# Layer 0's norm by DVE's statistics instructions, in a kernel of four graph attention layers

## The chip, the cores and the metric

The kernel runs on one core of a Trainium2 chip. The metric is the device time of that core in microseconds (us), as a median of several executions; lower is better. A core has five engines with a queue each, which they work off in order: TensorE (PE; its weight loads are listed apart as PEld), VectorE (DVE), ScalarE (ACT), GpSimd (POOL) and SyncE (SP, which issues DMAs). They wait for each other through semaphores.

## The reference

16 graphs of 1024 nodes with 256 features each go through four layers of graph attention. Each layer first normalizes the rows of x, cuts them at zero, projects them, forms attention weights over the edges, and adds the result to x. Cut to what matters here:

```python
def _layernorm(x, axis=-1, eps=1e-5):
    m = jnp.mean(x, axis=axis, keepdims=True)
    v = jnp.var(x, axis=axis, keepdims=True)
    return (x - m) / jnp.sqrt(v + eps)

# --- layer 0 (adj_preln) ---
h = jnp.maximum(_layernorm(x, axis=-1), 0.0)
x = x + _L0_gnn_ref(h, adj, L0_gnn_W, L0_gnn_a)
# layers 1, 2 and 3 have the same form, each with an attention of its own

# _L0_gnn_ref
Wh = jnp.einsum('bnf,fo->bno', h, W)
e = jax.nn.leaky_relu(f1[:, :, None] + f2[:, None, :], negative_slope=SLOPE)
e = jnp.where(adj == 0, NEG_INF, e)
attention = jax.nn.softmax(e, axis=-1)
h_prime = jnp.einsum('bij,bjo->bio', attention, Wh)
```

x is float32 of 16 x 1024 x 256, adj int32 of 16 x 1024 x 1024.

## The kernel before

A batch (one graph) is `xb`, 8 tiles of 128 nodes by 256 features, held in SBUF through all four layers. A layer has two parts. The projection (`project`, L267) works on a pair of tiles at a time: it finds the mean and the squares of each row, writes `centered` (row minus mean, cut at zero; the division by the deviation comes later), transposes it on TensorE (L290), copies it out of PSUM as `hT` on ACT (L292), multiplies it with W (L297), and hands each tile's product with `rstd`, the row's inverse deviation, to an eviction. The eviction of layers 0 and 1 takes an exponential on ACT (L361) and writes the values V on DVE (L365). The attention (`attend`, L393) transposes a column of V into a row (L314), makes eight tiles of weights of 128 x 1024 on DVE (L318), and multiplies them with V on TensorE (L409), two rows of results while the weights come and six afterwards. As results come (`finish0` L446, `add_elu` L336), x is updated on DVE with an instruction that also gives the row sums of the new x (`sums`), and every second tile starts the next layer's projection of that pair. So layers 1 to 3 get their sums along with the update. Layer 0 has no update ahead of it: `first` (L460) takes its sums from xb with a reduction of its own (L461), one over each pair.

From the sums, `project` makes `minus_mean` on DVE (L271), `centered` with it on DVE (L274), and the sum of squares on ACT (L281): a Square with the bias minus_mean, whose accumulator is read into `squared`. `inverse_root` (L257) adds the epsilon (L260) and raises to the power of -1/2 (L261), both on POOL. Layer 3 has four heads, whose sums are made with the weights as the moving operand (L517), copied (L579), turned back (L586, L594), and normalized again, head by head: L487 on POOL, L488 to L492 on DVE, the squares L494 on ACT, L496 on DVE, `inverse_root` on POOL, L500 on DVE, L501 and L502 on POOL; then the batch goes out (L611).

Two streams of batches run interleaved, the even ones and the odd ones. `stream` (L618) and the loop at L627 set the order of the text: each part yields a duration, and the stream with the least sum goes on; the second starts 111 units behind. So one stream's layer 3 and its next batch's layer 0 lie beside the other's layers 0 to 2. On each engine instructions keep the order that was fixed when the program was built; it need not be that of the text, save where `keep_in_program_order` says so.

Buffers are handed out by name: `minus_mean`, `squared`, `rstd2` and `sums_of_x` have six each, `centered` and `hT` three, `square` one, V four, x_b three. Except for the sums, all these names are shared by the layers and by both streams. The accumulators in PSUM (`acc0`, `acc1`) have two buffers for each stream. x_b is fetched by SP (L104), one megabyte a batch.

Of the kernel before, what the change touches and what calls it, by code (L numbers as in the profile page):

```python
# [32 lines left out]
F32 = mybir.dt.float32  # L33
BF = mybir.dt.bfloat16
# [3 lines left out]
AF = mybir.ActivationFunctionType  # L38
ALU = mybir.AluOpType
AX = mybir.AxisListType  # L40

P = 128
# [3 lines left out]
LN_EPS = 1e-5  # L46
# [13 lines left out]
def short_path(ctx: ExitStack, tc: tile.TileContext, ins: dict, out: bass.AP, bad: bass.AP):  # L60

    nc = tc.nc
    x, adj = ins["x"], ins["adj"]
    B, N, D = x.shape
    H, T, E = ins["L3_a_src"].shape
    NI = N // P
# [84 lines left out]
    work = ctx.enter_context(tc.tile_pool(name="work", bufs=3))  # L151
    small = ctx.enter_context(tc.tile_pool(name="small", bufs=6))
# [5 lines left out]
    bias = const.tile([P, D], F32, name="bias")  # L158
# [95 lines left out]

    def inverse_root(squared: bass.AP, n: int, elements: int, eps: float) -> bass.AP:  # L257

        r = small.tile([P, n], F32, name=f"rstd{n}")
        nc.gpsimd.tensor_scalar_add(r, squared, elements * eps)  # L260
        nc.gpsimd.tensor_tensor(r, r, minus_half.to_broadcast([P, n]), op=ALU.pow)  # L261
        return r

    def accumulator(b: int) -> bass.AP:
        return psum.tile([P, HALF], F32, name=f"acc{b % 2}")

    def project(b: int, l: int, xb: bass.AP, sums: bass.AP, pair: int, evict):  # L267


        minus_mean = small.tile([P, 2], F32, name="minus_mean")  # L270
        nc.vector.tensor_scalar_mul(minus_mean, sums[:, ts(pair, 2)], -1.0 / D)  # L271
        centered = work.tile([P, 2, D], F32, name="centered", bufs=3)
        for n in range(2):
            nc.vector.tensor_scalar(  # L274
                centered[:, n, :], xb[:, 2 * pair + n, :], minus_mean[:, n : n + 1], 0.0,
                op0=ALU.add, op1=ALU.max,
            )
        squared = small.tile([P, 2], F32, name="squared")
        for n in range(2):
            square = work.tile([P, D], BF, name="square", bufs=1)  # L280
            nc.scalar.activation(  # L281
                square, xb[:, 2 * pair + n, :], AF.Square, bias=minus_mean[:, n : n + 1],
                accum_out=squared[:, n : n + 1],
            )
        rstd = inverse_root(squared, 2, D, LN_EPS)
        yield 0.5
        turned = psum.tile([P, NK, 2 * P], F32, name="misc")
        for n in range(2):
            for k in range(NK):
                nc.tensor.transpose(turned[:, k, ts(n, P)], centered[:, n, ts(k, P)], ident)  # L290
        hT = wide.tile([P, NK, 2 * P], F32, name="hT", bufs=3)
        nc.scalar.mul(hT, turned, ROOT_D)  # L292
        yield 1.0
        for n in range(2):
            projected = accumulator(b)[:, : D + EXT[l]]
            for k in range(NK):
                nc.tensor.matmul(  # L297
                    projected, hT[:, k, ts(n, P)], W[l][:, k, :],
                    start=(k == 0), stop=(k == NK - 1),
                )  # L300
            evict(2 * pair + n, projected, rstd[:, n : n + 1])
        yield 2.5
# [46 lines left out]
    def batch(b: int):  # L349
        xb = xs.pop(b)  # L350
# [5 lines left out]
        def begin(l: int):  # L356

            V = nodes.tile([P, NI, H, E + 1], F32, name="V", bufs=4).rearrange("p i h e -> p i (h e)")

            def evict(i: int, projected: bass.AP, rstd: bass.AP):  # L360
                nc.scalar.activation(V[:, i, D : D + 3], projected[:, D:], AF.Exp, scale=rstd)  # L361
                if l == 2:
                    nc.scalar.mul(V[:, i, :D], projected[:, :D], rstd)
                else:
                    nc.vector.tensor_scalar(  # L365
                        V[:, i, :D], projected[:, :D], rstd, V[:, i, D : D + 1],
                        op0=ALU.mult, op1=ALU.mult,
                    )

            return V, evict  # L370
# [22 lines left out]
        def attend(l: int, V: bass.AP, finish, then: int):  # L393
# [35 lines left out]
            for i in range(NI):  # L429
                if i > 1:  # L430
                    for j in range(NI):
                        product(i, j)
                acc = accs.pop(i)
                finish(i, acc, sums[:, i : i + 1])
                if i != 0:
                    yield 3.6
                if i % 2 == 1:

                    yield from steps
                    steps = project(b, then, xb, sums, i // 2, following[1])  # L440
                yield from islice(steps, 1)
# [13 lines left out]
            add_elu(xb[:, i, :], acc, total)  # L455

        V, evict = begin(0)
        sums = small.tile([P, NI], F32, name="sums_of_x")

        def first(pair: int):  # L460
            nc.vector.tensor_reduce(sums[:, ts(pair, 2)], xb[:, ts(pair, 2), :], AX.X, ALU.add)  # L461
            yield from project(b, 0, xb, sums, pair, evict)

        pairs = [first(pair) for pair in range(NI // 2)]
        for n in range(NI // 2 + 2):
            for pair in range(max(n - 2, 0), min(n + 1, NI // 2)):
                yield from islice(pairs[pair], 1)
# [15 lines left out]
        def center(h: int):  # L483

            yh = y[:, :, h, :]
            head = ts(h, E)
            nc.gpsimd.tensor_add(yh, yh, bias[:, head].unsqueeze(1).to_broadcast(shape))  # L487
            nc.vector.scalar_tensor_tensor(yh, yh, 0.0, h3[:, :, head], op0=ALU.max, op1=ALU.add)  # L488
            mean = small.tile([P, NI], F32, name="mean")
            nc.vector.tensor_reduce(mean, yh, AX.X, ALU.add)  # L490
            nc.vector.tensor_scalar_mul(mean, mean, 1.0 / E)
            nc.vector.tensor_sub(yh, yh, mean.unsqueeze(2).to_broadcast(shape))  # L492
            square = wide.tile(shape, F32, name="wide", bufs=1)
            nc.scalar.activation(square, yh, AF.Square)  # L494
            var = small.tile([P, NI], F32, name="var")
            nc.vector.tensor_reduce(var, square, AX.X, ALU.add)  # L496
            return yh, head, inverse_root(var, NI, E, L3_EPS)
# [16 lines left out]
        def in_tiles(parts, accT: bass.AP, first: bool, last: bool):  # L514

            for n, (values, moving) in enumerate(parts):
                made = nc.tensor.matmul(  # L517
                    accT[ts(n, QUAD), :], values, moving, start=first, stop=last
                )

                if pinned:
                    tc.keep_in_program_order(made)
                pinned.append(made)
# [24 lines left out]
        for h in range(H):  # L548
# [16 lines left out]
            for first in range(0, NI, step):  # L565
                pinned = []
                for j in range(first, first + step, 2):
                    add_totals(h, j)
                    if h > 0:
                        add_values(h, j)  # L570
                for _ in range(step):
                    next(behind, None)
                yield 1.8 if h == 0 else 5.4
# [8 lines left out]
            sums, totals = copies if h == 0 else copies[::-1]  # L582
# [35 lines left out]
    def stream(first: int):  # L618
        for _ in loading[first]:
            yield 2.0  # L620
        for b in range(first, B, 2):
            yield from batch(b)
# [389 lines left out]
```

## Time and profile before

| What | Value |
|---|---|
| Median of three executions | 3025.95 us (3025.94 to 3026.56) |
| The profiled execution | 3025.06 us |
| Its span, first to last instruction | 3023.3 us |
| TensorE busy | 2905.2 us, 96% |
| DVE busy | 2112.7 us, 70% |
| ACT busy | 1092.1 us, 36% |
| POOL busy | 964.5 us, 32% |
| Mean granted TensorE clock | 0.993 |
| Layer 0's sums (L461) | 64 of 674 ns |
| minus_mean (L271), all layers | 256 of 189 ns |
| centered (L274), all layers | 512, median 347 ns |
| Squares (L281), all layers | 512 of 506 ns, and 512 accumulator reads of 191 ns |
| The two parts of inverse_root on POOL for 128x2 | 233 ns (L260) and 787 ns (L261) |

The profile is of one execution. Busy time is the time in which an engine works on an instruction; waits in its queue aren't counted. A group of instructions has its line, its engine, what it writes and reads, its count and mean duration; what stands in brackets behind an instruction in a timeline is the idle time of its engine ahead of it and what ended that. The chain that ended last is followed back from the last instruction, at each step to what released it. A quarter of each all-layer group belongs to layer 0.

### The profile page before, as it was taken

How to read it: one execution, taken by the hardware profiler on the slowest of the kernel's cores; microseconds unless marked ns; L12 is line 12 of the kernel's file. 1: busy time of each engine (PE TensorE's matmuls, PEld its weight loads, DVE VectorE, ACT ScalarE, POOL GpSimd, SP SyncE). 2: the span in 40 equal slices, each digit the busy share in tenths (PEclk: the TensorE clock that was granted, in tenths of full speed). 3: DMA queues.
4: the chain of work that ended last, by engine and by line, in shares of the span. 5: the costliest groups of instructions: out<-in, count | busy, mean ns of one | idle time of the engine just before them, and what ended most of it. 6: DMA issues, size and time to landing. Idle time of an engine off the chain costs nothing.

```text
span 3023.3 us, 44588 instructions
## 1 busy us (share of the span) xinstructions
PE 2905.2 (96%) x16774; PEld 1960.1 (65%) x16774; DVE 2112.7 (70%) x4467; ACT 1092.1 (36%) x3009; POOL 964.5 (32%) x1455
## 2 busy tenths in 40 slices
PE   7999999999999999999999999999999999999985
PEld 5775857658576675756758566585766857667551
DVE  5657687676866758677576875758667686675756
ACT  2333424243343433424334243433434334243331
POOL 2124324142232423324233242432324234242333
PEclk9999999999999999999999999999999999999997
DMA  7204023030321403122040220302204031110101
GB/s 122 37 8 63 29 29 56 8 49 29 36 49 14 71 2 49 36 28 57 5 50 31 29 56 8 50 29 32 53 11 56 19 50 36 15 29 5 19 21 30
DMA packets 120495, 106.11 MB, mean 35 GB/s; under 512 B 73680, under 2 KB 91216, under 8 KB 120272
## 3 DMA queue, kind: packets, MB, share of 16 engines
q0 software_dynamic: 40448, 67.12, 15.2%
q1 hardware_dynamic: 79824, 36.05, 5.9%
q8 instruction: 135, 2.21, 0.3%
q14 instruction: 88, 0.72, 0.1%
HBM read 153.49 MB, written 33.55 MB: 62 GB/s over the span
## 4 chain that ended last, share of the span: by engine, by line
PE 78%; DVE 12%; POOL 4%; ACT 4%; issue 2%; DMA 1%; SPq 0%; ACTq 0%; POOLq 0%; DVEq 0%
PE acc L409 39%; PE acc L517 21%; PE acc L297 11%; DVE weights L318 6%; PE misc L290 3%; PE row L314 2%; POOL rstd L261 2%; POOL y L487 1%; DVE y L500 1%; DVE V L365 1%; DVE var L496 1%; PE misc L594 1%; ACT adj_i L143 1%; ACT square L281 1%; PE misc L586 1%
## 5 line engine op out<-in xcount | busy, mean ns | idle before, releaser
L409 PE MATMUL acc<-V,weights 128*128 128x257 f32 x6144 | 1452.5, 386 | 24.6 <-ACT above L343 12.8
L409 PEld LDWEIGHTS acc<-V,weights 128*128 128x128 f32 x6144 | 1135.1, 190 | 338.3 <-DVE weights L318 92.7
L517 PE MATMUL acc<-weights,V 128*32 128x512 f32 x6144 | 756.4, 598 | 3.6 <-DVE weights L318 3.6
L318 DVE SCALAR_TENSOR_TENSOR weights<-row,ex,mask 128x1024 f32<-128x1024 f32 x512 | 631.2, 1276 | 91.0 <-PE acc L517 51.0
L297 PE MATMUL acc<-W,hT 128*128 128x259 f32 (+1 forms) x2048 | 522.1, 391 | 39.8 <-ACT hT L292 28.2
L297 PEld LDWEIGHTS acc<-W,hT 128*128 128x128 f32 x2048 | 376.5, 190 | 165.2 <-issue 49.5
L318 DVE SCALAR_TENSOR_TENSOR weights<-row,V,mask 128x1024 f32<-128x1024 f32 x384 | 475.4, 1276 | 7.7 <-PE row L314 7.7
L517 PEld LDWEIGHTS acc<-weights,V 128*32 128x32 f32 x6144 | 174.1, 109 | 379.6 <-issue 370.6
L341 ACT ACTIVATE below<-acc,inv 128x256 f32<-128x256 f32 x256 | 121.3, 474 | 681.0 <-DVE inv L334 404.1
L261 POOL TENSOR_TENSOR rstd<-rstd,minus_half 128x2 f32<-128x2 f32 (+1 forms) x320 | 307.7, 962 | 20.3
L281 ACT ACTIVATE square<-x_b,minus_mean 128x256 bf16<-128x256 f32 x512 | 259.2, 506 | 136.4 <-DVE minus_mean L271 131.7
L333 DVE TENSOR_SCALAR inv<-acc 128x1 f32<-128x1 f32 x256 | 39.7, 155 | 302.5 <-PE acc L409 299.0
L389 POOL TENSOR_TENSOR x_b<-x_b,beta 128x256 f32<-128x256 f32 x128 | 93.6, 731 | 491.1 <-ACT square L281 491.1
L579 ACT COPY sums<-acc 128x512 f32<-128x512 f32 x128 | 75.0, 586 | 413.9 <-PE acc L517 413.9
L260 POOL TENSOR_SCALAR rstd<-squared 128x2 f32<-128x2 f32 x256 | 59.5, 233 | 504.4 <-ACT square L281 503.6
L361 ACT ACTIVATE V<-acc,rstd 128x3 f32<-128x3 f32 x384 | 98.5, 262 | 315.2 <-PE acc L297 312.9
L292 ACT ACTIVATE hT<-misc 128x512 f32<-128x512 f32 x256 | 150.5, 594 | 155.4 <-PE misc L290 155.0
L365 DVE TENSOR_SCALAR V<-acc,rstd,V 128x256 f32<-128x256 f32 x256 | 133.1, 539 | 78.0 <-ACT V L361 77.2
L274 DVE TENSOR_SCALAR centered<-x_b,minus_mean 128x256 f32<-128x256 f32 x512 | 180.4, 383 | 4.3
L138 POOL DMA_DIRECT2D adj_i<-in_adj_dram x128 | 75.6, 590 | 331.0 <-ACT adj_i L143 262.2
L344 DVE SCALAR_TENSOR_TENSOR x_b<-below,x_b 128x256 f32<-128x256 f32 x256 | 117.7, 460 | 87.6 <-ACT below L341 87.4
L290 PE MATMUL misc<-ident,centered 128*128 128x128 f32 x1024 | 159.7, 278 | 15.7 <-DVE centered L274 13.8
(76 smaller groups left out, 2224.8 us busy)
## 6 DMA issues: line engine op xcount, KB each, us to landing
adj_i<-in_adj_dram POOLq DMA_DIRECT2D x128, 256.0 KB, 3.9
x_b<-in_x_dram SPq DMA_DIRECT2D x16, 1024.0 KB, 6.4
narrow<-in_adj_dram POOLq DMA_DIRECT2D x64, 256.0 KB, 9.5
out_dram<-y POOLq DMA_DIRECT2D x32, 512.0 KB, 7.5
mask<-narrow SPq DMA_TRANSPOSE x64, 4.3
W<-in_L_gnn_W_dram SPq DMA_DIRECT2D x3, 256.0 KB, 6.9
weights<-in_L_gnn_a_dram SPq DMA_DIRECT2D x3, 256.0 KB, 9.0
W<-in_L_gnn_W_dram SPq DMA_DIRECT2D x2, 128.0 KB, 7.9
```

What stands on the lines that cost most here:

```text
L261: nc.gpsimd.tensor_tensor(r, r, minus_half.to_broadcast([P, n]), op=ALU.pow)
L274: nc.vector.tensor_scalar(centered[:, n, :], xb[:, 2 * pair + n, :], minus_mean[:, n : n + 1], 0.0, op0=ALU.add, op1=ALU.max,)
L281: nc.scalar.activation(square, xb[:, 2 * pair + n, :], AF.Square, bias=minus_mean[:, n : n + 1], accum_out=squared[:, n : n + 1],)
L290: nc.tensor.transpose(turned[:, k, ts(n, P)], centered[:, n, ts(k, P)], ident)
L292: nc.scalar.mul(hT, turned, ROOT_D)
L297: nc.tensor.matmul(projected, hT[:, k, ts(n, P)], W[l][:, k, :], start=(k == 0), stop=(k == NK - 1),)
L318: nc.vector.scalar_tensor_tensor(w, r, c(j), masks[b][:, j // 2, :, j % 2], op0=op, op1=ALU.mult)
L341: nc.scalar.activation(below, acc[:, :D], AF.Exp, scale=inv)
L344: nc.vector.scalar_tensor_tensor(xi, below, 1.0, xi, op0=ALU.min, op1=ALU.add)
L365: nc.vector.tensor_scalar(V[:, i, :D], projected[:, :D], rstd, V[:, i, D : D + 1], op0=ALU.mult, op1=ALU.mult,)
L409: nc.tensor.matmul(accs[i], weights[j][:, ts(i, P)], V[:, j, : D + 1], start=(j == 0), stop=(j == NI - 1),)
L517: made = nc.tensor.matmul(accT[ts(n, QUAD), :], values, moving, start=first, stop=last)
```

## The change

For layer 0 alone, `project` is called with no sums. It then takes each tile of the pair by itself: `bn_stats` over its 256 elements and `bn_aggr` over the result write mean and variance of the rows into `mv`, both on DVE; `centered` subtracts the mean that stands there. The variance goes to `inverse_root`, which multiplies it by 256 and adds the epsilon in one instruction. The reduction L461, `minus_mean` and the squares on ACT are gone from layer 0; layers 1 to 3 keep theirs, but their `inverse_root` has the instruction with two operations too, with a factor of 1. `mv` and `stats` are new names with six buffers each.

```diff
-    def inverse_root(squared: bass.AP, n: int, elements: int, eps: float) -> bass.AP:
+    def inverse_root(squared: bass.AP, n: int, elements: int, eps: float, times=1.0) -> bass.AP:
         r = small.tile([P, n], F32, name=f"rstd{n}")
-        nc.gpsimd.tensor_scalar_add(r, squared, elements * eps)
+        nc.gpsimd.tensor_scalar(r, squared, times, elements * eps, op0=ALU.mult, op1=ALU.add)
         nc.gpsimd.tensor_tensor(r, r, minus_half.to_broadcast([P, n]), op=ALU.pow)
         return r
...
     def project(b: int, l: int, xb: bass.AP, sums: bass.AP, pair: int, evict):
-        minus_mean = small.tile([P, 2], F32, name="minus_mean")
-        nc.vector.tensor_scalar_mul(minus_mean, sums[:, ts(pair, 2)], -1.0 / D)
         centered = work.tile([P, 2, D], F32, name="centered", bufs=3)
+        if sums is None:
+            mv = small.tile([P, 2, nc.vector.BN_AGGR_DIM], F32, name="mv")
+            for n in range(2):
+                stats = small.tile([P, nc.vector.BN_STATS_DIM], F32, name="stats")
+                nc.vector.bn_stats(stats, xb[:, 2 * pair + n, :])
+                nc.vector.bn_aggr(mv[:, n, :], stats)
+                nc.vector.tensor_scalar(
+                    centered[:, n, :], xb[:, 2 * pair + n, :], mv[:, n, 0:1], 0.0,
+                    op0=ALU.subtract, op1=ALU.max,
+                )
+            rstd = inverse_root(mv[:, :, 1], 2, D, LN_EPS, D)
+        else:
+            minus_mean = small.tile([P, 2], F32, name="minus_mean")
+            nc.vector.tensor_scalar_mul(minus_mean, sums[:, ts(pair, 2)], -1.0 / D)
...
         V, evict = begin(0)
-        sums = small.tile([P, NI], F32, name="sums_of_x")
-
-        def first(pair: int):
-            nc.vector.tensor_reduce(sums[:, ts(pair, 2)], xb[:, ts(pair, 2), :], AX.X, ALU.add)
-            yield from project(b, 0, xb, sums, pair, evict)
-
-        pairs = [first(pair) for pair in range(NI // 2)]
+        pairs = [project(b, 0, xb, None, pair, evict) for pair in range(NI // 2)]
```

More of the change, by code (lines that the diff above doesn't have):

```diff
@@ L267, in project @@
     def project(b: int, l: int, xb: bass.AP, sums: bass.AP, pair: int, evict):
-        minus_mean = small.tile([P, 2], F32, name="minus_mean")
-        nc.vector.tensor_scalar_mul(minus_mean, sums[:, ts(pair, 2)], -1.0 / D)
         centered = work.tile([P, 2, D], F32, name="centered", bufs=3)
[L273 to L285, printed above, removed]
+        if sums is None:
[12 more added lines that the diff above has]
+            nc.vector.tensor_scalar_mul(minus_mean, sums[:, ts(pair, 2)], -1.0 / D)
+            for n in range(2):
+                nc.vector.tensor_scalar(
+                    centered[:, n, :], xb[:, 2 * pair + n, :], minus_mean[:, n : n + 1], 0.0,
+                    op0=ALU.add, op1=ALU.max,
+                )
+            squared = small.tile([P, 2], F32, name="squared")
+            for n in range(2):
+                square = work.tile([P, D], BF, name="square", bufs=1)
+                nc.scalar.activation(
+                    square, xb[:, 2 * pair + n, :], AF.Square, bias=minus_mean[:, n : n + 1],
+                    accum_out=squared[:, n : n + 1],
+                )
+            rstd = inverse_root(squared, 2, D, LN_EPS)
         yield 0.5
```

## The prediction

> **What bounds the kernel now.** I read the busy sums first, then the chain that ended last, then one period of the steady state cut into stretches, and last the engines' timelines in the stretch where TensorE stands idle. The busy sums and the chain's shares by engine:
>
> ```profile
> PE 2905.2 (96%) x16774; PEld 1960.1 (65%) x16774; DVE 2112.7 (70%) x4467; ACT 1092.1 (36%) x3009; POOL 964.5 (32%) x1455
> PE 78%; DVE 12%; POOL 4%; ACT 4%; issue 2%; DMA 1%; SPq 0%; ACTq 0%; POOLq 0%; DVEq 0%
> ```
>
> TensorE is busy 96% of the span; ACT has by far the most room of the engines that the change touches. The chain repeats every 184.0 us, one batch. One such period (us from the span's start, its length, then busy time of each engine):
>
> ```profile
> 974.00:1034.00 60.00, 59.37 (x381) 34.53 (x380) 45.08 (x90) 24.86 (x58) 25.56 (x30) 1.00 0.48 58
> 1034.00:1049.00 15.00, 12.43 (x70) 9.91 (x69) 11.90 (x34) 11.53 (x39) 9.03 (x13) 1.00 0.11 18
> 1049.00:1079.00 30.00, 29.83 (x142) 24.91 (x141) 27.04 (x57) 9.44 (x29) 9.11 (x17) 1.00 0.23 71
> 1079.00:1119.00 40.00, 40.00 (x194) 34.76 (x193) 14.13 (x56) 14.56 (x45) 11.23 (x25) 1.00 0.00 1
> 1119.00:1158.00 39.00, 39.00 (x270) 17.90 (x270) 32.97 (x42) 7.73 (x20) 4.91 (x9) 1.00 0.10 14
> ```
>
> TensorE idles 3.37 us of 184, and 2.57 of them in the second row, 1034 to 1049: there one stream ends layer 3 and begins its next batch's layer 0, the other ends its projection for layer 2. That is the stretch of layer 0's norm, and the only one where ACT is nearly full (11.53 of 15). The fourth row leaves DVE 25.9 us free. TensorE's idle moments in the stretch, then ACT before the first of them:
>
> ```profile
> 1042.25 1.04 PE L290 MATMUL misc<-ident,centered 128*128 128x128 f32 x8
> 1045.09 0.70 PE L297 MATMUL acc<-W,hT 128*128 128x259 f32 x2 [1.81 <-ACT hT L292]
> 1045.63 1.03 PE L409 MATMUL acc<-V,weights 128*128 128x257 f32 x4
> ...
> 1047.55 1.12 PE L297 MATMUL acc<-W,hT 128*128 128x259 f32 x4 [0.45 <-DVE V L365]
> ```
>
> ```profile
> 1042.80 0.63 ACT L494 ACTIVATE wide<-y 128x512 f32<-128x512 f32 x1 [1.05 <-DVE y L492]
> 1043.34 0.49 ACT L281 ACTIVATE square<-x_b,minus_mean 128x256 bf16<-128x256 f32 x1
> ...
> 1044.46 1.06 ACT L292 ACTIVATE hT<-misc 128x512 f32<-128x512 f32 x2
> ```
>
> TensorE waits 1.81 us for hT, which stands in ACT's queue behind two squares of layer 0. But the chain through the same stretch (start, length, what) runs elsewhere:
>
> ```profile
> 1037.89 0.73 POOL rstd L261
> 1038.62 1.38 POOL y L487
> ...
> 1044.57 1.67 POOL rstd L261
> 1046.23 0.02 issue
> 1046.26 0.69 DVE y L500
> 1046.95 0.46 DVE V L365
> 1047.40 2.38 DVE weights L318 x2
> ```
>
> It goes over POOL's queue and DVE's queue: layer 3's last head (L487 to L500), then the weights (L318) that L409 needs. Eight weights of 1.24 us each and the evictions L365 stand in DVE's order until 1056.66, and the matmuls L409 that follow end last.
>
> **What the Trainium skill says.** "Perfetto Trace Analysis", section "Optimizing Scalar/DVE Operations": if Scalar or DVE are not saturated but cause bubbles on other engines, breaking instructions up may let work be done sooner. The 1.81 us behind the squares is such a bubble, on an engine at 36%. "VectorE: DVE Perf Modes", section "Rules for kernel authors": keep the count of DVE operations low, and a reduction runs at the plain rate; the trace agrees, a reduction over 512 elements takes 674 ns and one over 256 takes 413. "GPSIMD Engine Reference", section 3.1: on GpSimd a body of up to two arithmetic operations an element is bound by its ports, so a second one should be free; no run here shows a two-operation instruction on POOL. No page prices the statistics instructions.
>
> **The change part by part, for one batch (four pairs of tiles).**
>
> Removed from DVE: 4 sums (L461) of 0.674 us and 4 minus_mean (L271) of 0.189, 3.45 us. Removed from ACT: 8 squares of 0.506 us and 8 accumulator reads of 0.191, 5.58 us, or 89 us over 16 batches: ACT's 1092.1 goes to about 1003.
>
> Added on DVE: 8 bn_stats over 256 elements and 8 bn_aggr over 6. The trace has neither. bn_stats: not under the 0.347 us of centered (L274, same shape), not over two reductions of 0.413; I take 0.41, one pass at the rate of a reduction. bn_aggr: not under a small operation (0.16, L334), not over 0.41; I take 0.17. Together 8 x 0.58 = 4.64 us, so DVE gains 1.2 us a batch, 19 us in all (low end 0.6, high end 6.4 us a batch). Centered keeps its form, with a subtraction from the mean.
>
> Where the added work lies decides. The order on an engine is not that of the text: L461 runs at 993 to 1013, while its minus_mean comes at 1035.7. For batch 1 L461 comes at 85.51, at once behind L345 at 84.82 to 85.25, the first to write the other stream's sums_of_x, though x_b had been asked for at 25.22 and DVE had stood idle for 2 to 3 us at a time between. I read this as: buffers of one name are handed out in the order of the text, and work moves forward as far as these allow. minus_mean and centered share their names with all layers and so stay behind the other stream's last pair. "mv" and "stats" are used by layer 0 alone, so they can go as soon as x_b lands: it is issued at 1050.15, lands 6.4 us later, and DVE's idle 25.9 us at 1079 to 1119 come next. There 4.64 us cost nothing; without this cover they cost what case D says. The sums leave 984 to 1014, where DVE is full but TensorE as well: no gain.
>
> inverse_root: L260 gets a multiplication in every layer, on 128x2 and 128x8, 233 and 275 ns. I take no change; the 42 ns that six more elements cost bound the other end, some 0.04 us each. The chain holds L261 for 2% of the span, 4 us a batch, so four or five such pairs a batch: 2.6 us in all at most.
>
> On the path: of the stretch at 1034 to 1049 four minus_mean leave, of which each takes 0.08 us of DVE's pitch (1035.62, 1035.70, 1035.77): 0.3 us. The squares leave ACT, so hT comes about 0.6 us earlier (two squares with their reads, 1043.34 to 1044.46, less the eviction L361 of 0.24 between and the wait for L494 to end). But what is late next is at hand: L409 can't start before the weights at 1045.34, the next projection needs the accumulator that L365 frees at 1047.4, and both are DVE's. So TensorE's earlier start is given back at the next wait; I count DVE's 0.3 us alone, in the 14 batches that begin behind another: 14 x 0.3 = 4.2 us. Start and end of the kernel: the first batch's norm runs beside the loads until 11 us, +1.2 us of DVE at most against 5.6 us of ACT less; counted at nothing.
>
> Profiled execution: 3025.06 us, of which the span is 3023.3. The median shown is 3025.95, 0.9 above it; I take the difference over to the median: 3025.95 - 4.2 = 3022.
>
> **The rivals.**
>
> B, the freed ACT opens the stretch: evictions (L361, then L365) also come earlier and take DVE's idle 0.92 us before L500, so that both waits of TensorE go. For it: L365's wait of 0.45 stands behind L361, and L361 behind a square. Against it: DVE's sum in the stretch doesn't fall. All of 2.26 us would give 14 x 2.26 = 32, 2994; half of it 3010.
>
> C, slower: POOL. The norm's rstd no longer waits for ACT. As soon as the other stream's last pair has its rstd (1037.58), those of layer 0 are ready, and a pair's L260 and L261 (0.22 + 0.73 to 1.02, with gaps 1.1 to 1.4 us) can stand ahead of L487 at 1038.60 or of L260 at 1044.24, both on the chain above. It decides once one pair stands there: 14 x 1.2 = 17, 3043; two pairs 3060. For it: POOL ran each of them where ACT's squares let it. Against it: L487 is ready at 1038.07, before POOL is free, and earlier in the text.
>
> D, slower: the statistics don't move forward but stand in the stretch, on DVE's chain: 4.64 - 0.32 = 4.3 us a batch, 14 x 4.3 = 60, 3086; half of them 3056.
>
> That nothing changes is excluded for ACT; for the time it is the edge of my main case.
>
> **How the numbers follow.** The main case, hidden statistics with small shifts of order: 0.46; its own range is -0.7 to +0.4 us a batch, 3016 to 3032. B 0.17, C 0.25, D 0.12. No change is what lies within 0.2%, 6 us, about what a measurement here can tell. Of the main case 0.17 is faster, 0.22 within, 0.07 slower. Faster: 0.17 + 0.17 = 0.34; same 0.22; slower 0.07 + 0.25 + 0.12 = 0.44. The range leaves out half of B below 3002 (0.08), and above 3058 three quarters of D (0.09) and what of C has two pairs (0.03): 3002 to 3058.
>
> **What would show it.** Right: bn_stats and bn_aggr far ahead of centered, outside 1034 to 1049 of the period; bn_stats at 0.41 and bn_aggr at 0.17; ACT near 1003 busy; the period 183.7 long. B: no wait of TensorE for hT left and a period between 181.8 and 182.9. C: L487 with an L261 of layer 0 right ahead. D: bn_stats between L274 and L318 in the stretch. I am wrong too if DVE waits for x_b to land under a bn_stats placed too early, or if the other streams' order on TensorE changes for reasons that none of this names.

## The result, and the profile after

The changed kernel takes 3096.33 us (median of five executions, 3095.82 to 3097.75) against 3025.94 us for the kernel before on the same chip: a ratio of 1.0235, with an interval of 1.0221 to 1.0249. It is slower by 70 us and lies above the forecast range. The profiled execution has a span of 3093.8 us (before 3023.3), and its mean granted TensorE clock is 0.978 (before 0.993).

The page of the changed kernel, its busy sums and the chain's shares by engine:

```profile
PE 2929.4 (95%) x16774; PEld 1984.3 (64%) x16774; DVE 2123.8 (69%) x4595; ACT 1031.1 (33%) x2753; POOL 939.4 (30%) x1455
PE 75%; DVE 12%; POOL 5%; ACT 4%; issue 2%; DMA 1%; SPq 0%; ACTq 0%; POOLq 0%; DVEq 0%
```

ACT lost 61 us and POOL 25, DVE gained 11. No engine took on 70 us of work; TensorE itself, with the same number of matmuls, is busy 24 us longer. So both waits and slower matmuls are to be looked for.

**Where the time went.** The issue of each batch's output (L617, before L611) serves as a milestone. The first comes at 329.88 us instead of 314.31: 15.6 us are lost at the start. From the first to the fourteenth it takes 2446.98 us instead of 2392.39: 54.6 us more, 188.2 a batch for 184.0. The rest of the span differs by 0.3 us. So there are two losses, one in each batch and one at the start. The first output already has one loss of the first kind behind it: with that loss mended (experiment 1) it comes at 326.59, so some 3.3 of the 15.6 us are the first kind and 12.3 the start's own.

**The loss in each batch.** One period of the changed kernel in stretches, as before (from and to, length, then the busy time of PE, PEld, DVE, ACT, POOL, each with its count, the granted clock, the DMA share and GB/s):

```profile
1003.50:1063.50 60.00, 59.38 (x381) 34.81 (x382) 43.47 (x86) 25.06 (x58) 25.23 (x30) 1.00 0.54 58
1063.50:1081.50 18.00, 13.16 (x64) 10.22 (x63) 10.56 (x29) 7.84 (x23) 8.87 (x15) 0.84 0.09 15
1081.50:1111.50 30.00, 29.83 (x141) 25.13 (x141) 29.48 (x69) 8.73 (x26) 7.00 (x11) 0.98 0.21 71
1111.50:1151.50 40.00, 40.00 (x194) 34.81 (x193) 14.77 (x57) 14.89 (x46) 12.52 (x27) 1.00 0.00 1
1151.50:1191.60 40.10, 40.10 (x275) 18.80 (x275) 33.52 (x46) 7.83 (x21) 4.88 (x9) 1.00 0.09 14
```

The second row answers to 1034 to 1049 of the kernel before. It is 18 us long, TensorE idles 4.84 us in it for 2.57, and the clock falls to 0.84. The others are nearly as they were. ACT is no longer full in it, and POOL's 8.87 us are no more than before: not the amount of work changed, but what stands where. TensorE's timeline there (start, length, group; in brackets the idle time ahead of it and what ended that):

```profile
1068.09 3.67 PE L309 MATMUL acc<-W,hT 128*128 128x259 f32 x16
1071.81 1.04 PE L302 MATMUL misc<-ident,centered 128*128 128x128 f32 x8
1077.17 3.82 PE L309 MATMUL acc<-W,hT 128*128 128x259 f32 x8 [4.33 <-ACT hT L304]
1081.19 1.78 PE L421 MATMUL acc<-V,weights 128*128 128x257 f32 x4 [0.19 <-DVE weights L330]
```

The wait of 1.81 us for hT has become one of 4.33. It isn't ACT's work that is late. The chain through the stretch (pieces of "issue" left out) and ACT's timeline show what came before:

```profile
1071.93 1.25 POOL y L493
1073.20 0.69 DVE y L494
...
1075.13 0.70 DVE y L498
1075.85 0.64 ACT wide L500
```

```profile
1076.53 1.07 ACT L304 ACTIVATE hT<-misc 128x512 f32<-128x512 f32 x2
```

hT (L304) stands in ACT's queue behind `wide` (L500), which waits for layer 3's last head, and that head stands behind five L261 on POOL. (The transposes that hT copies had ended at 1072.85; no run puts hT ahead of `wide`, so what this second order alone is worth isn't known.) POOL's timeline:

```profile
1067.14 0.19 POOL L260 TENSOR_SCALAR rstd<-squared 128x2 f32<-128x2 f32 x1 [4.99 <-ACT square L293]
1067.41 1.06 POOL L260 TENSOR_SCALAR rstd<-mv 128x2 f32<-128x2 f32 x4
1068.55 3.38 POOL L261 TENSOR_TENSOR rstd<-rstd,minus_half 128x2 f32<-128x2 f32 x5
1071.91 1.26 POOL L493 TENSOR_TENSOR y<-y,bias 128x512 f32<-128x512 f32 x1
```

Before, one L260 and one L261 ran ahead of this instruction (then L487):

```profile
1037.58 0.22 POOL L260 TENSOR_SCALAR rstd<-squared 128x2 f32<-128x2 f32 x1 [5.00 <-ACT square L281]
1038.60 1.39 POOL L487 TENSOR_TENSOR y<-y,bias 128x512 f32<-128x512 f32 x1
```

It was 1.02 us from the L260's start to its own. Now all four pairs of layer 0 have joined them, and it is 4.77 us: the head starts 3.75 us later. That is rival C of the prediction, with four pairs instead of one or two.

Not all of it is waiting. The same stretch in steps of 2 us, same columns:

```profile
1074.00:1076.00 2.00, 0.00 (x0) 0.00 (x0) 1.97 (x6) 0.15 (x1) 0.00 (x0) 0.93 0.00 0
1076.00:1078.00 2.00, 0.83 (x2) 0.73 (x3) 1.41 (x3) 1.60 (x4) 0.63 (x2) 0.50 0.00 0
1078.00:1080.00 2.00, 2.00 (x6) 1.52 (x6) 0.75 (x2) 0.26 (x1) 1.21 (x1) 0.50 0.00 0
1080.00:1082.00 2.00, 1.81 (x5) 0.98 (x4) 2.00 (x2) 0.26 (x1) 1.90 (x2) 0.50 0.00 0
1082.00:1084.00 2.00, 2.00 (x10) 1.64 (x10) 2.00 (x4) 0.00 (x0) 1.70 (x3) 0.87 0.04 15
```

While TensorE is still idle its granted clock falls to half, and it stays there for the first 5 us or so of matmuls: eight L309 take 3.82 us from 1077.17, where sixteen of the same shape took 3.67 from 1068.09. So it is in each of the 14 stretches of the changed kernel, for 6.8 us in twelve of them and 3.4 in two. "TensorE: Matmul & The Clock Gate", section "Part 1: The HAM clock gate", of the Trainium skill has the clock halved after an idle window of about 3.4 us. The trace agrees for the wait of 4.33 us, and the 1.81 us of the kernel before never halved it; but a wait need not be that long, since the 2.00 us of experiment 1 below halved it twice. Over a period of each kernel TensorE's idle time goes from 3.37 to 5.63 us (+2.26) and its busy time from 180.63 to 182.47 (+1.84, the half clock). Together that is the 4.1 us by which the two periods differ. Experiment 1 bears the second part out: with TensorE's order unchanged and its clock full, TensorE is busy 180.6 us a batch.

**The loss at the start.** DVE, SP's queue and TensorE between 50 and 100 us, one fence each:

```profile
82.18 0.22 DVE L345 TENSOR_SCALAR inv<-acc 128x1 f32<-128x1 f32 x2
94.03 0.43 DVE L275 BATCH_NORM_STATS2 stats<-x_b 128x6 f32<-128x256 f32 x1 [11.63 <-DMA x_b<-in_x_dram]
94.37 0.21 DVE L346 RECIPROCAL inv<-inv 128x1 f32<-128x1 f32 x2
```

```profile
51.72 35.41 SPq L124 DMA_TRANSPOSE mask<-narrow  x8
87.18 0.58 SPq L104 DMA_DIRECT2D x_b<-in_x_dram  x1
```

```profile
95.50 4.83 PE L421 MATMUL acc<-V,weights 128*128 128x257 f32 x12 [13.43 <-ACT above L355]
```

The third batch's first bn_stats (L275) stands on DVE between the two halves of batch 0's `inv` (L345, L346). Its x_b is fetched only at 87.18 us, since SP's queue holds eight mask transposes until then. DVE stands 11.63 us, the eviction behind L346 stands with it, and TensorE waits 13.43 us; its clock is halved from 85.9 to 99.5. In the kernel before, this x_b was fetched no earlier, but DVE never waited for it:

```profile
88.44 0.58 SPq L104 DMA_DIRECT2D x_b<-in_x_dram  x1
```

**What the statistics cost.** The new instructions by line (count, ns least/median/most, first and last start):

```profile
L275 DVE BATCH_NORM_STATS2 stats<-x_b x128: 393/409/428, 6.6 to 2603.2; 128x6 f32<-128x256 f32 x128
L276 DVE BATCH_NORM_AGGREGATE mv<-stats x128: 146/173/183, 7.3 to 2614.3; 128x2 f32<-128x6 f32 x128
```

409 and 173 ns, where the prediction took 410 and 170. In the steady state they run soon after x_b has come: for one batch, whose x_b was asked for at 894.57, at 903.6 to 909.5 us, while its `centered` (L277) comes in the next stretch, 1063.5 to 1081.5.

### The profile page after: what moved, and what is told of

Same layout as the page of the kernel before. It is cut to its first block, busy times and chain, and to the rows that moved or that the text cites. A ratio compares the mean times of both kernels' runs of the same rounds, so it can differ in the third digit from the quotient of the medians.

```text
span 3093.8 us, 44412 instructions
## 1 busy us (share of the span) xinstructions
PE 2929.4 (95%) x16774; PEld 1984.3 (64%) x16774; DVE 2123.8 (69%) x4595; ACT 1031.1 (33%) x2753; POOL 939.4 (30%) x1455
## 4 chain that ended last, share of the span: by engine, by line
PE 75%; DVE 12%; POOL 5%; ACT 4%; issue 2%; DMA 1%; SPq 0%; ACTq 0%; POOLq 0%; DVEq 0%
PE acc L421 39%; PE acc L523 21%; PE acc L309 10%; DVE weights L330 5%; POOL rstd L261 3%; PE misc L302 3%; PE row L326 2%; DVE stats L275 1%; POOL y L493 1%; DVE var L502 1%; DVE y L506 1%; ACT square L293 1%; POOL rstd L260 1%; DVE V L377 1%; DVE x_b L357 1%
## 5 line engine op out<-in xcount | busy, mean ns | idle before, releaser
L309 PE MATMUL acc<-W,hT 128*128 128x259 f32 (+1 forms) x2048 | 533.4, 402 | 69.1 <-ACT hT L304 63.2
L309 PEld LDWEIGHTS acc<-W,hT 128*128 128x128 f32 x2048 | 392.1, 197 | 191.1 <-ACT hT L304 69.3
L261 POOL TENSOR_TENSOR rstd<-rstd,minus_half 128x2 f32<-128x2 f32 (+1 forms) x320 | 288.3, 905 | 16.1
L345 DVE TENSOR_SCALAR inv<-acc 128x1 f32<-128x1 f32 x256 | 39.5, 155 | 310.4 <-PE acc L421 310.2
L293 ACT ACTIVATE square<-x_b,minus_mean 128x256 bf16<-128x256 f32 x384 | 194.4, 506 | 98.3 <-DVE minus_mean L284 77.8
L304 ACT ACTIVATE hT<-misc 128x512 f32<-128x512 f32 x256 | 150.7, 596 | 209.3 <-PE misc L302 209.1
L260 POOL TENSOR_SCALAR rstd<-squared 128x2 f32<-128x2 f32 x192 | 42.0, 219 | 442.3 <-ACT square L293 431.7
L302 PEld LDWEIGHTS misc<-ident,centered 128*128 128x128 f32 x1024 | 121.5, 142 | 73.5 <-issue 21.7
L356 DVE SCALAR_TENSOR_TENSOR x_b<-below,x_b 128x256 f32<-128x256 f32 x256 | 109.4, 427 | 73.7 <-ACT below L353 73.7
```

Source lines behind the costliest of these rows:

```text
L293: nc.scalar.activation(square, xb[:, 2 * pair + n, :], AF.Square, bias=minus_mean[:, n : n + 1], accum_out=squared[:, n : n + 1],)
L309: nc.tensor.matmul(projected, hT[:, k, ts(n, P)], W[l][:, k, :], start=(k == 0), stop=(k == NK - 1),)
L356: nc.vector.scalar_tensor_tensor(xi, below, 1.0, xi, op0=ALU.min, op1=ALU.add)
```

## The experiments

Theory P: POOL's order costs the 54.6 us of the steady state. Layer 0's L260 and L261 take their buffers under the name of all layers, `rstd2`, so they stay behind the other stream's last pair; since they no longer wait for squares on ACT, the order then puts them together, ahead of the head. Its rival is D in general: the statistics' own work on DVE costs the time, wherever it is. The start has a theory of its own: the statistics placed ahead of their data. The ratios below are to the kernel before on the same chip, where its median was 3023.8 to 3024.5; medians of different experiments can be a microsecond apart for that alone.

**1. Own buffers for layer 0's rstd.** The order on TensorE is the same as in the changed kernel. `mv` and `stats` get four buffers in place of six besides.

```diff
-    def inverse_root(squared, n, elements, eps, times=1.0):
-        r = small.tile([P, n], F32, name=f"rstd{n}")
+    def inverse_root(squared, n, elements, eps, times=1.0, name="rstd", bufs=6):
+        r = small.tile([P, n], F32, name=f"{name}{n}", bufs=bufs)
...
-            mv = small.tile([P, 2, nc.vector.BN_AGGR_DIM], F32, name="mv")
+            mv = small.tile([P, 2, nc.vector.BN_AGGR_DIM], F32, name="mv", bufs=4)
...
-                stats = small.tile([P, nc.vector.BN_STATS_DIM], F32, name="stats")
+                stats = small.tile([P, nc.vector.BN_STATS_DIM], F32, name="stats", bufs=4)
...
-            rstd = inverse_root(mv[:, :, 1], 2, D, LN_EPS, D)
+            rstd = inverse_root(mv[:, :, 1], 2, D, LN_EPS, D, "first", 4)
```

> The changed kernel, with layer 0's rstd under a buffer name of its own (first, four buffers; mv and stats get four each), so that its L260 and L261 on POOL can run as soon as the statistics are there, long before the stretch where the two streams meet. TensorE's order is that of the changed kernel. Theory P (POOL: four pairs of L260 and L261 stand ahead of the last head's y+bias, L493, and make TensorE wait 4.3 us a batch and lose its clock): the period falls from 188.1 to 183.0 to 184.3 us, the wait of 4.3 us is gone; the single wait of 13.4 us at the start stays, so 3030 to 3045. Rival D (the statistics on DVE, or the order that came with them, are what costs): the period stays above 187, 3085 or more.

Measured: 3045.87 us, ratio to the kernel before 1.0072 (1.0055 to 1.0089), a mean of 184.6 us a batch; both are just above what was expected. POOL's and TensorE's timelines at the same place:

```profile
1052.47 0.19 POOL L260 TENSOR_SCALAR rstd<-squared 128x2 f32<-128x2 f32 x1 [4.99 <-ACT square L293]
1052.75 0.75 POOL L261 TENSOR_TENSOR rstd<-rstd,minus_half 128x2 f32<-128x2 f32 x1
1053.45 1.40 POOL L493 TENSOR_TENSOR y<-y,bias 128x512 f32<-128x512 f32 x1
```

```profile
1058.86 2.02 PE L309 MATMUL acc<-W,hT 128*128 128x259 f32 x8 [0.69 <-ACT hT L304]
1062.88 1.13 PE L421 MATMUL acc<-V,weights 128*128 128x257 f32 x4 [2.00 <-DVE weights L330]
1064.18 1.83 PE L421 MATMUL acc<-V,weights 128*128 128x257 f32 x4
```

Under a name of their own the four pairs' rstd move ahead to the statistics, and the head comes 0.98 us after the L260 again. The wait of 4.33 us is gone, and with it most of the half clock, but not all. In this very stretch the clock falls once more, behind the wait of 2.00 us:

```profile
1064.00:1066.00 2.00, 2.00 (x9) 1.53 (x7) 2.00 (x4) 0.00 (x0) 1.70 (x3) 0.57 0.41 15
```

It does so in two of the 14 stretches, for 3.4 us each, and these two batches take 185.2 us where the others take 184.5. Set against the kernel before on its chip, 21 of the 70 us are left: some 49 are POOL's order, with the half clock that came of it. The wait at the start stays, with 14.17 us.

**2. The aggregates held back.** `mv` becomes a slice of one tile for each batch, under the name that the sums had.

```diff
-            mv = small.tile([P, 2, nc.vector.BN_AGGR_DIM], F32, name="mv")
+            mv = moments[:, ts(pair, 2), :]
...
+        moments = small.tile([P, NI, nc.vector.BN_AGGR_DIM], F32, name="sums_of_x")
```

> The changed kernel, with mean and variance in one tile a batch under the name sums_of_x, the name that held layer 0's sums before. Theory of the names (buffers of one name are handed out in the order of the text): the statistics move back to where L461 stood, some 25 to 45 us ahead of centered; the wait for x_b at 82 to 94 us goes, 11 to 14 us. Theory P: rstd stays where it is, so the period stays at 188 and the time is 3080 to 3087. Rival D (early statistics are what costs a batch 4 us): the period goes back to 184, 3025 to 3035.

Measured: 3091.45 us, 1.0221 (1.0204 to 1.0238), 188.1 us a batch. POOL, and then DVE at the start:

```profile
1063.50 3.38 POOL L261 TENSOR_TENSOR rstd<-rstd,minus_half 128x2 f32<-128x2 f32 x5
1066.86 1.26 POOL L494 TENSOR_TENSOR y<-y,bias 128x512 f32<-128x512 f32 x1
```

```profile
94.18 0.43 DVE L275 BATCH_NORM_STATS2 stats<-x_b 128x6 f32<-128x256 f32 x1 [7.94 <-DMA x_b<-in_x_dram]
```

Where the aggregates stand is of no effect on the five L261 ahead of the head, as P has it. The start was missed: it was to recover, and TensorE's wait fell to 5.93 us only. The bn_stats write to "stats", which has six buffers of its own, so they were not held back and DVE still waits 7.94 us for x_b.

**3. The two-operation L260 alone,** in the kernel before, whose order is unchanged.

```diff
-        nc.gpsimd.tensor_scalar_add(r, squared, elements * eps)
+        nc.gpsimd.tensor_scalar(r, squared, 1.0, elements * eps, op0=ALU.mult, op1=ALU.add)
```

> The kernel before, with L260 alone changed to the form with multiplication (by 1.0) and addition; every engine's order is that of before. Expected: L260 at 0.20 to 0.24 us for 128x2, no change of time, 3024 to 3028. Rival (a second operation costs POOL some 40 ns): 3028 to 3030.

Measured: 3020.16 us (20 executions), below what was expected, 0.9990 (0.9983 to 0.9996), a mean of 183.8 us a batch. L260 by form in the kernel before, then in this one (ns least/median/most):

```profile
L260 POOL TENSOR_SCALAR rstd<-squared x256: 208/224/598, 9.2 to 2928.4; 128x2 f32<-128x2 f32 x128
L260 POOL TENSOR_SCALAR rstd<-var x64: 240/247/741, 238.5 to 3003.3; 128x8 f32<-128x8 f32 x64
```

```profile
L260 POOL TENSOR_SCALAR rstd<-squared x256: 183/193/1008, 9.3 to 2926.4; 128x2 f32<-128x2 f32 x128
L260 POOL TENSOR_SCALAR rstd<-var x64: 192/198/697, 238.7 to 3002.5; 128x8 f32<-128x8 f32 x64
```

The second operation doesn't cost; the instruction gets 31 and 49 ns shorter. That part of the change is worth some 3 us of gain, and this is the only version here that is faster than both kernels, by 0.1%.

**4. Mean from the statistics, variance from ACT's squares.** All of the statistics stay on DVE; only what feeds POOL goes back to ACT.

```diff
-            rstd = inverse_root(mv[:, :, 1], 2, D, LN_EPS, D)
+            minus_mean = small.tile([P, 2], F32, name="minus_mean")
+            nc.vector.tensor_scalar_mul(minus_mean, mv[:, :, 0], -1.0)
+            squared = small.tile([P, 2], F32, name="squared")
+            for n in range(2):
+                square = work.tile([P, D], BF, name="square", bufs=1)
+                nc.scalar.activation(
+                    square, xb[:, 2 * pair + n, :], AF.Square, bias=minus_mean[:, n : n + 1],
+                    accum_out=squared[:, n : n + 1],
+                )
+            rstd = inverse_root(squared, 2, D, LN_EPS)
```

> The changed kernel, with the mean from the statistics as before, but the variance from ACT's squares again (and minus_mean from the mean that the statistics give). L260 of layer 0 waits for ACT's squares again, and stands behind the last head's y+bias. Theory P: the period goes back to 183.7 to 184.6, the wait at the start stays: 3033 to 3046. Rival D: DVE now carries the statistics and four minus_mean, more than in the changed kernel, and nothing is better: 3090 or more.

Measured: 3033.55 us, 1.0029 (1.0018 to 1.0041), a mean of 183.8 us a batch, as good as the kernel before (184.0). POOL:

```profile
1049.83 0.76 POOL L261 TENSOR_TENSOR rstd<-rstd,minus_half 128x2 f32<-128x2 f32 x1
1050.53 1.41 POOL L502 TENSOR_TENSOR y<-y,bias 128x512 f32<-128x512 f32 x1
1052.02 0.69 POOL L260 TENSOR_SCALAR rstd<-squared 128x2 f32<-128x2 f32 x1
```

The head (here L502) is back in its place, and layer 0's L260 comes after it. The eight bn_stats and eight bn_aggr are still there, far ahead of the stretch, and each batch takes no longer than before, nor than the 183.8 of experiment 3, which has the same L260 and none of the statistics: the rival falls. Only the start's wait, 13.73 us here, is left.

**5. The mirror: mean from sums, variance from the statistics.**

```diff
+        minus_mean = small.tile([P, 2], F32, name="minus_mean")
+        nc.vector.tensor_scalar_mul(minus_mean, sums[:, ts(pair, 2)], -1.0 / D)
...
-        if sums is None:
+        if l == 0:
...
-                nc.vector.tensor_scalar(
-                    centered[:, n, :], xb[:, 2 * pair + n, :], mv[:, n, 0:1], 0.0,
-                    op0=ALU.subtract, op1=ALU.max,
-                )
             rstd = inverse_root(mv[:, :, 1], 2, D, LN_EPS, D)
...
+            nc.vector.tensor_reduce(sums[:, ts(pair, 2)], xb[:, ts(pair, 2), :], AX.X, ALU.add)
```

> The mirror of the run with ACT's squares: layer 0's mean from the sums L461 as in the kernel before, and only the variance from the statistics instructions, so that the squares leave ACT and rstd no longer waits for them. Theory P: again four pairs stand ahead of the last head's y+bias on POOL, period 187.5 to 188.5, and the statistics of the third batch wait for x_b at the start: 3080 to 3100. Rival (the new way to the mean, or its place, is what costs): period 184, 3025 to 3045.

Measured: 3102.31 us, 2 us above what was expected, 1.0262 (1.0245 to 1.0279), a mean of 188.5 us a batch; five L261 take 3.38 us ahead of the head again. Together with the run before it this splits the change in two: not the mean from the statistics but the variance from them, on its way to POOL, costs the steady state its 4 us.

**6. Own rstd, and the third batch's bn_stats held to the text's order.** The first experiment, and this:

```diff
+                made = nc.vector.bn_stats(stats, xb[:, 2 * pair + n, :])
+                if b == 2:
+                    tc.keep_in_program_order(made)
```

> The run with rstd under its own name, and with the third batch's statistics kept to their place in the text, so that none of them stands ahead of the x_b that is still to come. Theory S (the wait of 14.2 us for x_b at the start is a cost of its own and adds to the rest): 3030 to 3036, 10 to 15 us under the run without it, with no wait of TensorE over 2 us between 80 and 100 us.

Measured: 3036.84 us, 1.0043 (1.0026 to 1.0060): 8 to 9 us less than the first experiment, a mean of 184.6 us a batch from the second output on. DVE where it had waited:

```profile
82.49 0.21 DVE L347 TENSOR_SCALAR inv<-acc 128x1 f32<-128x1 f32 x2
82.67 0.23 DVE L348 RECIPROCAL inv<-inv 128x1 f32<-128x1 f32 x2
```

The reciprocals follow at once, and TensorE has no wait above 2 us there. The first output comes 14.1 us earlier than in the first experiment (312.51 for 326.59). Some of it is given back: to the second output it takes 189.6 us for 184.5, with waits of 2.71 and 0.99 us of TensorE at 306 to 311 and half its clock for 6.8 us, so the time is just above what was expected.

**7. The fourth experiment with the same holding.** The edit is that of the two together.

> The run with the mean from the statistics and ACT's squares, and with the third batch's statistics kept to their place in the text. If P and S are all there is, nothing of the 70 us is left: period 183.8 as with the two operations on POOL alone, 3018 to 3024, no slower than the kernel before. If the statistics on DVE cost anything of their own, it stays above 3026.

Measured: 3025.85 us (12 executions), 1.0007 (0.9998 to 1.0016): no difference from the kernel before can be told. A mean of 183.8 us a batch from the second output on; again one spacing, from the first output to the second, is long (190.9 us), which is why it isn't the few us faster that were expected. Still it accounts for the loss: with the variance fed from ACT and the third batch's statistics after their data, nothing of the 70 us is left against the kernel before. Against experiment 3, whose L260 it shares, some 5 us are left; the one long spacing is 7 us longer than the others. It is not the change repaired, since the squares are back on ACT; with them gone, experiment 6 is the best, 13 us slower than the kernel before.

**8. The statistics in the stretch.** The first experiment, with the bn_stats written to buffers under the name `minus_mean`, so that they stay behind the other stream's pairs: case D by itself, save that the order on TensorE changes with it.

```diff
-                stats = small.tile([P, nc.vector.BN_STATS_DIM], F32, name="stats", bufs=4)
+                stats = small.tile([P, nc.vector.BN_STATS_DIM], F32, name="minus_mean")
```

> The run with rstd under its own name, but with the statistics under the name minus_mean that the other layers use, so that they come behind the other stream's last pair, into the stretch where the streams meet. This is the prediction's case D by itself. Expected by its price: 4.3 us a batch if all of it falls on DVE's chain there, period 186.5 to 189, 3070 to 3100 (the wait for x_b at the start should go, 13 us, as the statistics come later). If DVE has room there after all: period under 185.5.

Measured: 3069.65 us, 1.0148 (1.0131 to 1.0165), a mean of 187.1 us a batch, as expected. DVE in the stretch, with some of the statistics between the head's instructions and the weights:

```profile
1053.27 0.39 DVE L275 BATCH_NORM_STATS2 minus_mean<-x_b 128x6 f32<-128x256 f32 x1
1057.67 0.69 DVE L506 TENSOR_TENSOR y<-y,rstd 128x512 f32<-128x512 f32 x1 [1.58 <-POOL rstd L261]
1058.28 3.66 DVE L330 SCALAR_TENSOR_TENSOR weights<-row,V,mask 128x1024 f32<-128x1024 f32 x3
1061.95 0.40 DVE L275 BATCH_NORM_STATS2 minus_mean<-x_b 128x6 f32<-128x256 f32 x1
```

With the statistics there a batch takes 2.5 us more (187.1 less the 184.6 of experiments 1 and 6). TensorE's own order differs too, so not all of it need be the statistics; its clock is not the reason, for it halves in only five of the 14 stretches (behind waits of 1.90 us), and a batch where it doesn't still takes 187.0. So the cover that the prediction named is real: outside the stretch the statistics cost nothing (experiment 4), inside it up to 2.5 us. The start's wait is gone here as well, since the statistics no longer run ahead of their data.

**9. Layer 0's centered on ACT.** The sixth experiment, with the freed ACT in use: does DVE's work in the stretch hold the 184.6 us?

```diff
-                nc.vector.tensor_scalar(
-                    centered[:, n, :], xb[:, 2 * pair + n, :], mv[:, n, 0:1], 0.0,
-                    op0=ALU.subtract, op1=ALU.max,
-                )
+            nc.vector.tensor_scalar_mul(mv[:, :, 0], mv[:, :, 0], -1.0)
+            for n in range(2):
+                nc.scalar.activation(
+                    centered[:, n, :], xb[:, 2 * pair + n, :], AF.Relu, bias=mv[:, n, 0:1]
+                )
```

> A way to use the freed ACT: the run with rstd under its own name and the third batch kept in its place, with layer 0's centered on ACT (Relu with the bias minus mean, about 0.5 us each) in place of DVE (eight of 0.26 us pitch). If DVE's chain in the stretch bounds the period, as the prediction held, 2 us of it go: period 182 to 183.5, 3000 to 3022. If the order on ACT or the last head's chain over POOL bounds it: period at 184.4 or above, 3033 or more.

Measured: 3040.0 us, 1.0053 (1.0036 to 1.0069), a mean of 184.7 us a batch from the second output on: the second of the two cases expected. Eight instructions fewer on DVE in the stretch gain nothing. TensorE's waits there are shorter (0.99 us the longest), but it is busy 181.5 us a batch for 180.6, in another order; why isn't shown. What still stands there is the head's own chain, POOL's L261 of 1.65 us and the weights behind L509.

**What stays open.** With layer 0's own rstd buffers a batch takes 184.5 us (185.2 where the clock halves), with the squares on ACT 183.8. The order on TensorE differs between the two, and so does DVE's: the kernel before puts one of the weights (1044.07, 1.27 us) into the time in which it else waits for L261 ahead of the head's L500, and in the first experiment DVE idles 1.60 us at that place and all weights follow behind L506. That this is the cause of the 0.7 us was read, not tried. Nor was it shown why the first spacing becomes 5 to 7 us longer in experiments 6, 7 and 9.

## Why the prediction was wrong

**The step that failed** is the sentence against rival C: "L487 is ready at 1038.07, before POOL is free, and earlier in the text". It argues as if POOL chose among what is ready when it comes free, or took the text's order. Neither holds: the order on POOL is fixed, and the prediction itself had noted that it isn't the text's. So layer 0's rstd, taken off ACT's squares, went ahead of the head: 4.77 us from the first L260 to the head's instruction in place of 1.02, and some 49 of the 70 us. The main case counted nothing for it. C's mechanism was right, place included; experiments 1, 4 and 5 show it. Its size was cut off at two pairs without a reason in the profile, though layer 0 has four and all are ready alike. By its own rate four pairs give 14 x 4 x 1.2 = 67 us, 3093. That this lies so near the 3096.33 is in part chance: four pairs delay the head by 3.75 us, not 4.8; 1.84 of the 4.1 us a batch are the half clock, which no case named; and some 12 us of the total are the start's.

**The start was named and not priced.** "If DVE waits for x_b to land under a bn_stats placed too early" is what happened, once, in the third batch; the 11.63 us wait had its place among what would make the prediction wrong but none in the sum or the range. "Start and end of the kernel: ... counted at nothing" looked at the first batch alone. What was overlooked is in the trace of before: there too SP's queue fetches the third x_b at 88.44 us. The prediction used it that "mv" and "stats" let the statistics move forward, but not that their data can be late. The same freedom to move, counted as free cover, was also the hazard. Experiment 6 puts its price at 8 to 9 us net.

**Statistics hidden: right.** They moved forward as far as their own names allow; not into the free 40 us at 1079 to 1119 but to the landing of x_b, and cost nothing a batch there (experiment 4: 183.8 us). The prices of 0.41 and 0.17 us were right to 3 ns.

**DVE's and ACT's sums: sizes off.** DVE gained 11 us for 19 (0.7 us a batch, near the low end of 0.6 that was named), ACT lost 61 for 89. A square and its accumulator read overlap: in the kernel before they start 0.4 us apart, and a square takes 0.506. Busy time counts the overlap once, 61 / 128 = 0.48 us a square; adding the two durations counted it twice.

**B did not come.** ACT became free in the stretch (7.84 us busy in 18 for 11.53 in 15), and no wait went away for it; even with POOL's order mended (experiment 1) 0.69 and 2.00 us are left, and the batch is no shorter than before.

**D: mechanism right, size off.** With the statistics in the stretch a batch takes 3.1 us more than before (187.1 for 184.0) where 4.3 were forecast. The sum took each instruction at its full length, 0.58 us a tile, but on DVE they overlap with what follows: in experiment 8 a bn_aggr starts at 1053.18, the bn_stats after it at 1053.27, the next instruction at 1053.58. That is 0.40 us a tile, 3.2 a batch. Against experiment 1 it is 2.5; of what is missing there, 0.24 us is a wait of L502 that is filled, and the rest isn't accounted for.

**L260 "no change": wrong in sign.** The bounds looked upward only, at +42 ns; it is 31 ns shorter. "GPSIMD Engine Reference", section 3.1, of the Trainium skill has bodies of up to two operations bound by their ports, from which the prediction took a second one to be free. Experiment 3 agrees that it isn't slower; why it is faster, no run here shows.

## What to carry to other kernels

Work that no longer waits for another engine can turn up earlier in its own queue: for each instruction that a change makes ready sooner, look at what stands behind it there, and count all of its copies, not one. Which names share buffers tells how far such work moves, and that cuts both ways: a name shared with others kept the rstd together at the worst place, and a name of its own let the statistics run ahead of their data at the start. Price a delay of a busy TensorE twice: as a wait, and, where the wait can cost it its clock (here at times from 1.9 us on, and each time at 4.33), as slower matmuls behind it.

## What the runs showed of the hardware

On POOL, an addition of a constant over 128x2 took 224 ns (median) and the same with a multiplication ahead of it 193 ns; over 128x8 it was 247 and 198. Around waits of 4.33 us TensorE's granted clock fell to 0.50 in all 14 stretches of the changed kernel, for 3.4 or 6.8 us; behind waits of 2.00 us it did so in two of 14 (experiment 1), behind 1.90 in five of 14 (experiment 8), each time for 3.4 us, and behind the 1.81 to 1.84 us of the kernel before in none of 14.
